# Order of TensorE's products in a fused attention and octonion-FFN block: a planner by runs of one kind, a third p buffer, and ternary signs on ScalarE

## The chip, the cores and the metric

The kernel runs on one core of a Trainium2 chip. The metric is the device time of one execution in microseconds, as the median of several runs. Engines are called by the names of the profile: PE (TensorE's products) and PEld (its weight loads), DVE (VectorE), ACT (ScalarE), POOL (GpSimd) and SP (SyncE, which only issues DMAs here).

## The reference, cut to what matters

Two batches of 1024 tokens with 512 features are normalised once. One branch is a 32-head causal attention with ALiBi, the other an FFN whose three weight matrices are made ternary and expanded by the signs of octonion multiplication. Their product is added to x.

```python
xn = layernorm(x)                                   # x: (2, 1024, 512)
q, k, v = split(xn @ w_qkv.T + b_qkv)               # 32 heads of 16
scores = q @ k.T / 4 + slope[h] * position[k]       # causal: later keys -1e9
s = (softmax(scores) @ v) @ w_out.T + b_out

scale = mean(|W|)                                   # for w_gate, w_up, w_down
Wq = scale * clip(round(W / scale), -1, 1)
M[k, o, i, d] = sum_j S_OCT[j, i, k] * Wq[j, o, d]  # S_OCT has 0, 1 and -1
h = silu(xn @ M_gate) * (xn @ M_up)                 # 1360 wide
g = silu(h @ M_down)
out = x + s * g
```

## The kernel before, in words

**Head (to about 150 us).** Eight tiles of x are loaded by SP, then wv, the FFN weights and eight more tiles. DVE normalises a tile, PE transposes it into PSUM (L358) and ACT copies it to xnT (L359). Meanwhile the FFN weights are made ternary: DVE sums |W| (L264), PE adds over partitions (`tot`, L270), DVE compares with half the scale (L282, L283). For each of the three weights and four slabs `kt`, `expand` (L285 to L304) multiplies by signs: four TENSOR_TENSOR of 340 columns on POOL (L296) into one of two tiles m. `expand_in` then writes m to the DRAM tensor mw by two DMAs that POOL issues (L310, L314); `expand_down` leaves m to PE's transposes (`turn_down`, L328), and ACT copies them on.

**Attention (about 150 to 950 us).** A unit is one batch, one group of four heads and one half of the queries; there are 32 units. Five kinds of product run on PE:
- projections: `pqk` (L433) for q and k, `pv` (L390) for v, `pout` (L667). In fp32, two MATMUL records for one product. q and k are split into a high and a low part, spilled to DRAM and filled back by SP into the rings of tiles q_stack and k_stack.
- scores for the maximum (L501): queries on partitions, 126 rows, into one of two PSUM tiles of pool `ps_x`. DVE reduces each to its row maximum (L511, L514).
- `place_max` (L546): the unit's maxima are transposed by PE, rounded by ACT into `mr` (L553), and written into the last two rows of q_stack by four DMAs that POOL issues (L555). So the next score product subtracts the maximum by itself.
- scores for the exponential (L575): keys on partitions, into one of three PSUM tiles of `ps_e`. On the diagonal a bf16 product of an identity and a mask is added (L584), at once after the score. ACT takes the exponential into p (L585). A cell is one unit and one block of 128 keys, with four heads, so four scores and one tile p.
- value products (L598): p times v, in column tiles of 32, one for each head; a step is the four heads of one cell, eight MATMUL records. At a unit's end `posb`, a transpose (L618) and the normalisation follow.

**Order.** All PE instructions stand in the order in which the program writes them (`pe`, a helper); the tile framework orders the other engines. A planner at build time writes the order: a loop (L927 to L1077) keeps a clock `now`, modelled times of ACT and DVE (`run_act`, `run_dve`), and when PSUM tiles come free (`e_free`, `x_free`, `m_free`). Each round, every source of work (row maxima to place, normalisations, value steps, projections in `side`, FFN transposes in `behind`, scores for the maximum, scores for the exponential) offers its next piece with a ready time and a rank; the earliest wins, and the rank decides among those ready within 60 ns. A change from one kind to another costs nothing in the model. An exponential may be at most one cell ahead of the value steps. Costs are columns times 0.45 to 0.5.

**FFN (from about 953 us).** A fixed loop over four blocks of 512 tokens and eleven slabs `mt`: `gate_up` (L1127), ACT's silu into sg (tag oT), DVE's product h, `down` (L1161), and at each block's end four evictions `ga` (tag mr). The expanded weights come from mw into tiles `fw`, which take over tiles of the attention.

Of the kernel before, what the change touches and what calls it, by code (L numbers as in the profile page):

```python
# [10 lines left out]
F32 = mybir.dt.float32  # L11
# [48 lines left out]
def kernel(  # L60
# [33 lines left out]
    pp = ctx.enter_context(tc.tile_pool(name="pp", bufs=2))  # L94
# [55 lines left out]
    wv_sb = wqp.tile([P, KD, D], F32, tag="wv", name="wv_sb")  # L150
# [25 lines left out]
    nc.sync.dma_start(out=wv_sb, in_=wv.rearrange("(k p) n -> p k n", p=P))  # L176
# [108 lines left out]
    def expand(name, kt, dtype):  # L285

        w = w_tiles[name]
        signs = sgn["d" if name == "d" else "i"]
        m = tmp.tile([P, 8, H8], dtype, tag="m", name=f"m_{name}_{kt}")

        def blocks(t):
            return t.rearrange("p (a b c) o -> p a b c o", a=2, b=2)

        for a in range(2):
            for b in range(2):
                nc.gpsimd.tensor_tensor(  # L296
                    blocks(m)[:, a, b],
                    blocks(w)[:, a ^ (kt // 2), b ^ (kt % 2)],
                    signs[:, kt, 4 * a + 2 * b : 4 * a + 2 * b + 2]
                    .rearrange("p (c o) -> p c o", o=1)  # L300
                    .to_broadcast([P, 2, H8]),
                    ALU.mult,
                )
        return m  # L304
# [72 lines left out]
    def v_items(b, hh):  # L377
# [3 lines left out]
        def product(kt, c):  # L381
# [4 lines left out]
            if c == 0:  # L386
# [6 lines left out]
                    rhs=wv_sb[:, c, hh * 256 : (hh + 1) * 256],  # L393
# [3 lines left out]
            )  # L397
            if c == KD - 1:
                nc.vector.tensor_tensor(  # L399
                    v_tiles[b, hh][:, kt, 0 : 16 * VC].rearrange("p (h e) -> p h e", e=VC)[  # L400
                        :, :, 0:HD
                    ],
                    ps[:, 0:256].rearrange("p (h d) -> p h d", d=HD),
                    bv_sb[:, hh * 256 : (hh + 1) * 256].rearrange("p (h d) -> p h d", d=HD),
                    ALU.add,
                )

        return [
            (1024, lambda kt=kt, c=c: product(kt, c), "v" if c == KD - 1 else None)
# [4 lines left out]
    def qk_items(b, gp):  # L414
# [3 lines left out]
        def product(which, c, kt):  # L418
# [38 lines left out]
            (2048, lambda w=w, c=c, kt=kt: product(w, c, kt), "qk" if kt == KD - 1 else None)  # L457
# [82 lines left out]
    def place_max(b, g, qc, tiles):  # L540
# [11 lines left out]
        mr = wk.tile([8, 512], F32R, tag="mr", name=f"mr_{b}_{g}_{qc}")  # L552
# [12 lines left out]
    def exp_step(b, g, qc, kt, i):  # L565
# [17 lines left out]
        if kt >= 4 * qc:  # L583
            pe(nc.tensor.matmul(ps[:, 0:P], lhsT=ident16, rhs=mask16, start=False, stop=True))  # L584
# [52 lines left out]
    def out_items(b, qc):  # L637
# [53 lines left out]
        for t in range(4 * qc, 4 * qc + 4):  # L691
            if t % 4 == 0:
                items.append((512, lambda t=t: turn(t), "t"))
            if t % 4 < 3:
                items.append((512, lambda t=t: go_on(t), "t"))
            for c in range(KD):
                items.append(
                    (2048, lambda t=t, c=c: product(t, c), "out" if c == KD - 1 else None)
                )
# [111 lines left out]
    def weight(name, last):  # L811
# [6 lines left out]
        later(lambda: ternary_total(name), None, ("s", name), 128)  # L818
# [4 lines left out]
        for kt in range(4):  # L823
# [4 lines left out]
            for f in range(0, NM if last else 0, 4):  # L828
                later(lambda kt=kt, f=f: turn_down(kt, f), None, ("e", name, kt), 512, "t")

    def more_tokens(ts):
        for t in ts:
# [4 lines left out]
            later(lambda t=t: norm_item(t), None, ("n", t), 512, "t")  # L837
# [25 lines left out]
    put([(512, lambda t=t: norm_item(t), "t", ("n", t)) for t in range(4)])  # L863
    put(qk[0:4] + qk[8:12])
    put([(512, lambda t=t: norm_item(t), "t", ("n", t)) for t in range(4, 8)])
# [15 lines left out]
    now = [0.0]  # L881
# [5 lines left out]
    turns, norms = [], []  # L887
    HELD = 1e12
    S_ = [0]

    def take(pool):
        pool.sort()
        return pool

# [32 lines left out]
    while E[0] < len(exps) or V[0] < len(vals) or S_[0] < len(side) or norms or behind:  # L927
        try_fill()
        try_fetch()
# [6 lines left out]
        best = None  # L936

        def offer(ready, rank, go):
            nonlocal best
            start = max(ready, now[0])  # L940
            key = (start if start > now[0] + 60 else now[0], rank)
            if best is None or key < best[0]:
                best = (key, start, go)


        if turns:
            u, ready = turns[0]

            def go(u=u):
                turns.pop(0)  # L950
                place_max(*units[u], mtiles[u])
                now[0] += 500
                take(m_free)[0] = run_act(now[0] + 100, 600)
                placed[u] = m_free[0] + 3500

            offer(max(ready, min(m_free)), 0, go)
        if norms:
            u, ready = norms[0]

            def go(u=u):  # L960
                norms.pop(0)
                normalise(*units[u])
                now[0] += 500
                take(m_free)[0] = run_dve(now[0] + 100, 600)
                stored[units[u]] = m_free[0] + 5000

            offer(max(ready, min(m_free)), 1, go)

        if V[0] < len(vals) and vals[V[0]] in p_ready and (V[0] or S_[0] >= head_v):
            u, kt = vals[V[0]]  # L970

            def go(u=u, kt=kt):
                value_step(*units[u], kt)
                V[0] += 1
                now[0] += 4 * width(units[u][2], kt) * 0.5
                if kt == 4 * units[u][2] + 3:
                    o_free[0] = run_act(now[0] + 100, 600)
                    norms.append((u, o_free[0] + 100))

            vready = p_ready[u, kt] + 100  # L980
            if kt == 0:
                vready = max(vready, o_free[0])
            offer(vready, 2, go)

        if S_[0] < len(side):
            due, ok, (cost, emit, kind, *need) = side[S_[0]]
            if ok():

                def go(cost=cost, emit=emit, kind=kind):
                    emit()  # L990
                    S_[0] += 1
                    now[0] += cost * 0.45
                    if kind == "none":
                        return
                    if HELD not in m_free:
                        take(m_free)[0] = HELD
                    if kind is None:
                        return
                    if kind == "v":
                        end = run_dve(now[0] + 100, 450)  # L1000
                    elif kind == "qk":
                        end = run_dve(run_act(now[0] + 100, 700), 750)
                        done_qk[0] += 1

                        if done_qk[0] == 2 or done_qk[0] % 4 == 0:
                            qk_done.append(end + 4000)
                    elif kind == "t":
                        end = run_act(now[0] + 100, 600)
                    else:
                        end = run_dve(now[0] + 100, 700)  # L1010
                    m_free[m_free.index(HELD)] = end

                t = 0 if HELD in m_free or not cost else min(m_free)
                for k in need:
                    t = max(t, known[k] + 100)
                offer(t, 3 if pos >= due else 6, go)

        while behind and not behind[0][3] and known.get(behind[0][2], 0) <= now[0]:
            emit, model = behind.pop(0)[:2]
            emit()  # L1020
            if model:
                model()
        if behind and behind[0][3]:
            emit, model, need, cost, kind = behind[0]

            def go(emit=emit, cost=cost, kind=kind):
                behind.pop(0)
                emit()
                now[0] += cost * 0.45
                if kind == "t":  # L1030
                    take(m_free)[0] = run_act(now[0] + 100, 600)

            offer(max(known[need] + 100, 0 if HELD in m_free else min(m_free)), 4.5, go)

        if M[0] < len(maxs):
            u, n, count, cost, emit = maxs[M[0]]
            g = u // 2
            if fills[0] > 4 * g + 1 + 2 * units[u][2] and (n or u < 2 or u - 2 in placed):
                mpos = at[u] + (at[u + 1] - at[u]) * n / count

                def go(u=u, n=n, count=count, cost=cost, emit=emit):
                    emit()
                    M[0] += 1
                    now[0] += cost * 0.46
                    end = run_dve(now[0] + 100, cost * 1.1 + 190)
                    take(x_free)[0] = end
                    if n == count - 1:
                        split_max(*units[u], mtiles[u])
                        turns.append((u, run_dve(end, 400) + 100))

                lead = size[1] + size[0] * 0.6
                rank = 4 if mpos < pos + lead else 5.5
# [235 lines left out]
```

## Time and profile before

| | |
|---|---|
| median of 3 runs | 1231.95 us (1231.39 to 1234.6) |
| profiled execution | 1228.66 us |
| its span, first to last instruction | 1226.9 us |
| granted PE clock over the span | 0.963 |
| L585, exponentials on ACT, x768 | 332.2 us busy |
| L501, scores for the maximum, x768 | 312.3 us busy |
| L575, scores for the exponential, x768 | 255.5 us busy |
| L598, value products, x1536 | 166.4 us busy |
| L433, q and k projections, x256 | 137.0 us busy |
| L584, masks, x512 | 115.6 us busy |
| L555, DMAs of the maxima, issue to landing | 1.6 us median |
| L310, DMAs of the expanded weights | 5.3 us median |

The page gives for each engine its busy time, share of the span and number of instructions; a chain of work that ended last; and groups of equal instructions. A line of the timeline has the start and the length in us, the engine, the line of the kernel, the operation, output and inputs by name, and the shapes. Times of one line overlap with those of the next: PE's ends are modelled, and a product's record may start while its weights are still being loaded. Intervals between starts are therefore more telling than lengths.

### The profile page before, as it was taken

To read this page: it belongs to the slowest core of one execution; us is meant where nothing else is said; L and a number is where in the kernel's file an instruction comes from. 1 tells how busy PE (TensorE), PEld (TensorE's weight loads), DVE (VectorE), ACT (ScalarE), POOL (GpSimd) and SP (SyncE) were. 2 spreads that over 40 slices of the span, in tenths; PEclk is the share of its full clock that TensorE was granted. 3 is DMA by queue.
4 is the path that set the end of the run, shared out by engine and by line. 5 is a ranking of instruction groups with operands and counts; after the bars stand their busy time and mean duration, and the time that the engine had idled before them with its cause. 6 is when DMAs were issued, how large, how long until landed. Compare 5 with 4: busy or idle time off the path is not lost.

```text
span 1226.9 us, 16539 instructions
## 1 busy us (share of the span) xinstructions
PE 1117.5 (91%) x5714; PEld 671.7 (55%) x5714; DVE 617.5 (50%) x1640; ACT 487.0 (40%) x1035; POOL 272.8 (22%) x446
## 2 busy tenths in 40 slices
PE   4757689989999999998999999999888999999997
PEld 2534445544455555545555554455444677777775
DVE  6684327656666665665655655666641113232122
ACT  1113252445546445453544534455453212222222
POOL 6697430200210110012001000100110113232222
PEclk9887889999999998999999999999889999999999
DMA  9963484163544152533616332652316110203020
GB/s 277 239 191 121 132 118 93 36 114 54 129 64 69 47 127 47 90 75 92 97 60 114 53 88 50 141 81 49 108 49 205 44 61 14 89 9 95 9 95 35
DMA packets 76788, 112.31 MB, mean 92 GB/s; under 512 B 29424, under 2 KB 30960, under 8 KB 76704
## 3 DMA queue, kind: packets, MB, share of 16 engines
q1 hardware_dynamic: 67120, 93.05, 34.2%
q0 software_dynamic: 9296, 17.16, 5.0%
q8 instruction: 45, 0.74, 0.3%
q10 hardware_dynamic: 288, 1.05, 0.2%
q14 instruction: 39, 0.32, 0.1%
HBM read 72.71 MB, written 37.98 MB: 90 GB/s over the span
## 4 chain that ended last, share of the span: by engine, by line
PE 76%; DMA 7%; POOL 6%; issue 6%; DVE 3%; ACT 2%; SPq 0%; DVEq 0%; POOLq 0%; ACTq 0%
PE s L501 14%; PE s L575 13%; PE po L598 12%; PE pg L1127 7%; PE pqk L433 6%; PE pu L1127 6%; PE pd L1161 6%; PE pout L667 4%; DMA q_stack<-mr 4%; PE s L584 3%; PE pv L390 2%; DVE scr L514 1%; PE pm L546 1%; POOL m_g L296 1%; PE pt L618 1%
## 5 line engine op out<-in xcount | busy, mean ns | idle before, releaser
L585 ACT ACTIVATE p<-s 128x512 f32<-128x512 f32 (+3 forms) x768 | 332.2, 493 | 323.2 <-PE s L584 174.6
L501 PE MATMUL s<-k_stack,q_stack 126*128 126x512 f32 (+3 forms) x768 | 312.3, 448 | 6.3 <-DVE mx L514 4.2
L575 PE MATMUL s<-q_stack,k_stack 128*128 128x512 f32 (+3 forms) x768 | 255.5, 391 | 32.0 <-DMA q_stack<-mr 30.2
L501 PEld LDWEIGHTS s<-k_stack,q_stack 126*128 126x128 f32 x768 | 138.4, 194 | 164.6 <-DVE mx L514 74.1
L511 DVE TENSOR_REDUCE mp<-s 128x1 f32<-128x512 f32 x256 | 170.2, 688 | 81.9 <-PE s L501 80.1
L514 DVE CUSTOM_DVE_ANT_0 scr<-s,mask,mp 128x128 f32<-128x128 f32 (+3 forms) x256 | 140.7, 550 | 106.7 <-PE s L501 93.1
L575 PEld LDWEIGHTS s<-q_stack,k_stack 128*128 128x128 f32 x768 | 151.0, 199 | 70.1 <-DMA q_stack<-mr 35.0
L555 POOL DMA_DIRECT2D q_stack<-mr x128 | 63.9, 505 | 520.4 <-ACT mr L553 455.2
L514 DVE CUSTOM_DVE_ANT_0 scr<-s,mask 128x128 f32<-128x128 f32 (+3 forms) x256 | 125.2, 489 | 91.6 <-PE s L501 74.4
L598 PE MATMUL po<-p,v 128*32 128x512 f32 (+3 forms) x1536 | 166.4, 502 | 0.0
L433 PE MATMUL pqk<-xnT,wq 128*128 128x512 f32 x256 | 137.0, 637 | 16.3 <-ACT mr L553 10.6
L1138 DVE SCALAR_TENSOR_TENSOR h<-pu,sc_u,sg 128x512 f32<-128x512 f32 (+1 forms) x44 | 33.0, 750 | 166.1 <-PE pu L1127 156.3
L584 PE MATMUL s<-mask,ident 128*128 128x128 bf16 x512 | 115.6, 231 | 0.0
L1144 POOL TENSOR_TENSOR hs<-h,hs 128x512 fp32r<-128x512 f32 (+1 forms) x44 | 56.9, 1293 | 197.2 <-ACT hs L1143 197.2
L584 PEld LDWEIGHTS <-ident 128*128 128x128 bf16 x512 | 49.4, 96 | 56.9 <-issue 37.4
L390 PE MATMUL pv<-wv_sb,xnT 128*128 128x256 f32 x256 | 72.6, 395 | 2.6 <-DVE v L399 1.2
L433 PEld LDWEIGHTS pqk<-xnT,wq 128*128 128x128 f32 x256 | 47.2, 203 | 41.5 <-issue 19.5
L1136 ACT ACTIVATE sg<-pg,sc_g 128x512 f32<-128x512 f32 (+1 forms) x44 | 30.3, 688 | 97.9 <-PE pg L1127 97.8
L667 PE MATMUL pout<-wo_sb,oT 128*128 128x512 f32 x128 | 62.4, 602 | 1.7 <-ACT oT L658 1.0
L598 PEld LDWEIGHTS po<-p,v 128*32 128x32 f32 x1536 | 31.4, 108 | 58.0 <-issue 51.5
L1143 ACT CAST hs<-h 128x512 fp32r<-128x512 f32 (+1 forms) x44 | 27.3, 621 | 77.7 <-DVE h L1138 74.9
L390 PEld LDWEIGHTS pv<-wv_sb,xnT 128*128 128x128 f32 x256 | 45.1, 194 | 13.6 <-issue 4.5
(147 smaller groups left out, 1127.0 us busy)
## 6 DMA issues: line engine op xcount, KB each, us to landing
sp<-st SPq DMA_DIRECT2D x32, 512.0 KB
k_stack<-sp SPq DMA_DIRECT2D x128, 128.0 KB
q_stack<-sp SPq DMA_DIRECT2D x128, 128.0 KB
wqr<-in_wqk_dram POOLq DMA_DIRECT2D x14, 512.0 KB, 6.1
xt<-in_x_dram SPq DMA_DIRECT2D x16, 256.0 KB
att<-o SPq DMA_DIRECT2D x32, 128.0 KB
ot<-att SPq DMA_DIRECT2D x16, 256.0 KB
proj<-y SPq DMA_DIRECT2D x16, 256.0 KB
```

What stands on the lines that cost most here:

```text
L390: nc.tensor.matmul(ps[:, 0:256], lhsT=xnT[:, c, b * S + kt * P : b * S + (kt + 1) * P], rhs=wv_sb[:, c, hh * 256 : (hh + 1) * 256], start= ...
L433: nc.tensor.matmul(ps, lhsT=wq_tiles[b, gp][:, kt, which, :], rhs=xnT[:, kt, b * S + c * 512 : b * S + (c + 1) * 512], start=(kt == 0), st ...
L501: nc.tensor.matmul(ps[:, :n], lhsT=q_of(b, g, qc)[0 : NR - 2, i, tl * P : (tl + 1) * P], rhs=k_of(b, g, c)[0 : NR - 2, i, :n], start=True, ...
L511: nc.vector.tensor_reduce(pm, ps, AX.X, ALU.max)
L514: nc.vector.tensor_tensor_reduce(out=scr[:, :n], in0=ps[:, :n], in1=mask[:, 512 - n : 512], scale=1.0, scalar=pm if qc else -3.0e38, op0=A ...
L575: nc.tensor.matmul(ps[:, :w], lhsT=k[0:NR, i, kt % 4 * P : (kt % 4 + 1) * P], rhs=q[0:NR, i, 512 - w : 512], start=True, stop=(kt < 4 * qc),)
L584: pe(nc.tensor.matmul(ps[:, 0:P], lhsT=ident16, rhs=mask16, start=False, stop=True))
L585: nc.scalar.activation(p_tiles[b, g, qc, kt][:, i, :w], ps[:, :w], AF.Exp, scale=0.25)
L598: nc.tensor.matmul(po[32 * i : 32 * i + 32, 512 - w : 512], lhsT=v[:, kt, h * VC : h * VC + 32], rhs=pr[:, i, :w], start=(kt == 0), stop=( ...
L667: nc.tensor.matmul(ps, lhsT=turned[t][:, c, :], rhs=wo_sb[:, c, :], start=(c == 0), stop=(c == KD - 1),)
L1127: nc.tensor.matmul(ps[:fs, :], lhsT=fw[mt][:, n0 + kt, 0:fs], rhs=part[:, kt, :], start=(kt == 0 and n == 0), stop=(kt == KD - 1 and n == 1),)
L1161: nc.tensor.matmul(pd, lhsT=hs[k][:fs, n, st * P : (st + 1) * P], rhs=fw[mt][:fs, 8:12, :].rearrange("p s n -> p (s n)"), start=(mt == 0 a ...
```

## The change

Edits that the text speaks of:
- PE's kinds get letters: R (both scores), V (value), F (fp32), B (bf16 mask). A table SWITCH charges changes of kind. Costs are set anew (858 for a 512-column projection product in place of 2048 times 0.45, and so on).
- The planner goes on with scores while one can start soon. When none can, it writes all masks that are pending, and only then their exponentials. Then come value steps and other work, with a budget RUN for side work, before the next scores.
- A value step of even key block waits in the model for the next cell too, so that two steps come together. The exponentials may be two cells ahead, and p has three tiles.
- `expand` is eight ACTIVATEs with the sign as scale, of 170 columns, on ACT.
- wv is loaded in halves of 256 columns, four times in all, into one buffer; the next half is issued after the last product that reads the one before.
- `mr` has one buffer, `ga` takes the tag oT, and the third FFN weight tile takes over a p tile.

```diff
-    pp = ctx.enter_context(tc.tile_pool(name="pp", bufs=2))
+    pp = ctx.enter_context(tc.tile_pool(name="pp", bufs=3))
...
-    wv_sb = wqp.tile([P, KD, D], F32, tag="wv", name="wv_sb")
+    wv_tiles = {}
+    def load_wv(n):
+        w = wqp.tile([P, KD, D // 2], F32, tag="wv", name=f"wv_{n}")
+        nc.sync.dma_start(
+            out=w,
+            in_=wv.rearrange("(k p) n -> p k n", p=P)[:, :, n % 2 * 256 : n % 2 * 256 + 256],
+        )
+        wv_tiles[n] = w
...
-        for a in range(2):
-            for b in range(2):
-                nc.gpsimd.tensor_tensor(
-                    blocks(m)[:, a, b],
-                    blocks(w)[:, a ^ (kt // 2), b ^ (kt % 2)],
-                    signs[:, kt, 4 * a + 2 * b : 4 * a + 2 * b + 2]
-                    .rearrange("p (c o) -> p c o", o=1)
-                    .to_broadcast([P, 2, H8]),
-                    ALU.mult,
-                )
+        for k in range(8):
+            nc.scalar.activation(
+                m[:, k, :], w[:, k ^ kt * 2, :], AF.Identity, scale=signs[:, kt, k : k + 1]
+            )
...
+            if (kt, c) == (7, KD - 1) and 2 * b + hh < 2 * B - 1:
+                load_wv(2 * b + hh + 1)
...
-        if kt >= 4 * qc:
-            pe(nc.tensor.matmul(ps[:, 0:P], lhsT=ident16, rhs=mask16, start=False, stop=True))
+        return ps
+
+    def mask_step(ps):
+        pe(nc.tensor.matmul(ps[:, 0:P], lhsT=ident16, rhs=mask16, start=False, stop=True))
+
+    def exp_of(b, g, qc, kt, i, ps):
+        w = width(qc, kt)
         nc.scalar.activation(p_tiles[b, g, qc, kt][:, i, :w], ps[:, :w], AF.Exp, scale=0.25)
...
+    SWITCH = {
+        ("R", "V"): 95,
+        ("F", "V"): 95,
+        ("B", "V"): 95,
+        ("V", "R"): 200,
+        ("V", "F"): 100,
+        ("V", "B"): 95,
+        ("R", "B"): 60,
+        ("F", "B"): 95,
+        ("B", "R"): 105,
+        ("B", "F"): 50,
+    }
+    SOON = 80
+    RUN = 1800
...
+    def run_pe(k, ready, cost):
+        now[0] = max(ready, now[0] + SWITCH.get((kind[0], k), 0)) + cost
+        kind[0] = k
...
+    def next_exp():
...
+        if u not in placed or V[0] < E[0] // 4 - 2:
+            return []
...
+        def go():
+            ps = exp_step(*units[u], kt, i)
+            E[0] += 1
+            run_pe("R", ready, max(width(units[u][2], kt) * 0.417 + 18, 108))
+            take(e_free)[0] = HELD
+            if kt < 4 * units[u][2]:
+                after(ps)
+            else:
+                masks.append((ps, after))
...
+    def next_value():
...
+        if kt % 2 == 0 and E[0] < len(exps) and E[0] // 4 < V[0] + 3:
+            ready = max(ready, p_ready.get((u, kt + 1), HELD) - 800)
+        return [(ready, 0, 0, go)] if ready < HELD else []
...
+        def soon(found):
+            return [f for f in found if f[0] <= now[0] + SOON and f[1] < 7]
+
+        scores = next_max(pos) + next_exp()
+        scores.sort(key=lambda f: (max(f[0], now[0] + SOON), f[1]))
+        if kind[0] == "R" and soon(scores):
+            scores[0][3]()
+            return True
+        if masks:
+            run_pe("B", 0, 60)
+            ps, after = masks.pop(0)
+            mask_step(ps)
+            after(ps)
+            return True
+        rest = next_value() + next_turn() + next_side(pos) + next_behind()
+        rest.sort(key=lambda f: (max(f[0], now[0] + SOON), f[1]))
+        if soon(rest) and (left[0] > 0 or not soon(scores)):
+            left[0] -= rest[0][2]
+            rest[0][3]()
+            return True
+        left[0] = RUN
+        found = soon(scores) or scores + rest
...
-        wqp.tile([P, 12, P], F32R, tag="wv", name="fw_2"),
+        pp.tile([P, 4, 512], F32R, tag="p", name="fw_2"),
...
-            ga = wk.tile([P, D], F32, tag="mr", name=f"ga_{n}")
+            ga = wk.tile([P, D], F32, tag="oT", name=f"ga_{n}")
```

## The prediction

> **What bounds the kernel now.** I read the page first, then the stretches of 100 us, PE's waits, and the timeline of PE alone.
>
> ```profile
> span 1226.9 us, 16539 instructions
> PE 1117.5 (91%) x5714; PEld 671.7 (55%) x5714; DVE 617.5 (50%) x1640; ACT 487.0 (40%) x1035; POOL 272.8 (22%) x446
> ...
> PE 76%; DMA 7%; POOL 6%; issue 6%; DVE 3%; ACT 2%; SPq 0%; DVEq 0%; POOLq 0%; ACTq 0%
> ```
>
> ```profile
> 0.00:100.00 100.00, 61.15 (x199) 36.89 (x199) 70.91 (x138) 17.26 (x37) 74.08 (x161) 0.88 0.84 234
> ...
> 300.00:400.00 100.00, 98.29 (x596) 53.67 (x594) 68.81 (x202) 53.06 (x121) 13.06 (x27) 1.00 0.52 92
> ```
>
> The columns of the second fence are the stretch, then PE, PEld, DVE, ACT and POOL busy. PE is the bound from about 150 us on; the first 150 us are a chain of several engines. DVE at 69 and ACT at 53 of 100 us have room. But a busy PE is not a PE multiplying: the timeline shows what passes between its products.
>
> ```profile
> 303.57 0.33 PE L575 MATMUL s<-q_stack,k_stack 128*128 128x384 f32 x1
> 303.75 0.23 PE L584 MATMUL s<-mask,ident 128*128 128x128 bf16 x1
> 303.79 0.42 PE L575 MATMUL s<-q_stack,k_stack 128*128 128x384 f32 x1
> 304.05 0.23 PE L584 MATMUL s<-mask,ident 128*128 128x128 bf16 x1
> 304.21 1.07 PE L598 MATMUL po<-p,v 128*32 128x512 f32 x8
> 305.20 0.61 PE L501 MATMUL s<-k_stack,q_stack 126*128 126x384 f32 x2
> 305.65 0.34 PE L575 MATMUL s<-q_stack,k_stack 128*128 128x384 f32 x1
> 305.83 0.23 PE L584 MATMUL s<-mask,ident 128*128 128x128 bf16 x1
> ```
>
> Durations overlap in these records, so I use steps from start to start. I name the kinds E (score for the exponential, L575), M (score for the maximum, L501), B (mask, L584), V (value, L598) and F (projections and transposes).
> - **A mask.** From mask to mask over one 384-wide E: 304.05 − 303.75 = 0.30 us. A 384-wide M or E without a mask behind it takes 0.177 (the short steps of these products). So E's companion costs 0.123 us, where its own 128 columns are about 0.06 (a quarter of the 0.235 step of 512 columns, below): 0.063 is change of kind.
> - **A value step.** Its second pass starts 0.45 after the first, and all its columns need 0.86. Over the whole trace, the median from the product before to the second pass is 0.115 us more than the products themselves, and from the last pass to the second product after it 0.216 us more. Together 0.33 us per visit to V.
> - **M after M** never steps below 0.335 us at 512 columns; E after E steps at 0.235 (median of 133). So 0.104 us each.
>
> From 150 to 935 us (785 us) the products alone, at their undisturbed steps, are 270 (M, E) + 178 (F) + 130 (V) + 30 (B) = 608. Add 188 visits to V × 0.33 = 62, 496 masks × 0.063 = 31, 215 × 0.104 = 22, and 41 of waits that the wait view lists: 764. Only 21 us stay unexplained. The largest wait is
>
> ```profile
> PE s L575 <- DMA q_stack<-mr: 23.5, 8, 6.2
> ```
>
> **What the Trainium skill says.** TensorEngine Tiling (Array Packing), Key Properties: a change of tiling mode drains TensorE. V runs in 32-column tiles, everything else on the full array; the 0.33 us agrees. TensorE: Matmul & The Clock Gate, Step-by-step: weight loads are pulled ahead of running matmuls. E after E (0.235) agrees, M after M (0.335) doesn't show it. ScalarE: Activation LUTs, What ACT_TABLE_LOAD costs: an ACTIVATE takes 186 ns + 0.833 per element, 93 more per pointer operand, and neighbours overlap by 93; four 512-wide exponentials in 2.08 us (0.52 each) agree. GPSIMD Engine Reference, Specifications: it shares SBUF interfaces with VectorE; at 74.39 us a 128x16 CAST on DVE (L537) takes 5.35 us beside POOL's memset and sign products, which fits.
>
> **The change, part by part.** The built program's order of PE can be counted, before against after. The products are the same: 768 M, 768 E, 512 B, 768 V, 751 F.
> 1. *Visits to V* fall from 192 (always one step) to 103 (89 of two steps). 89 × 0.33 = 29.4 saved; two steps in one visit keep a pass-to-pass step, 89 × 0.021 = 1.9. Net −27.5. They lie on PE, the bound; nothing else covers them.
> 2. *Runs of masks* fall from 512 to 217 (134 of three). 295 changes go. A mask behind a mask isn't in this trace: at best 0.053 us (128 columns), at worst 0.107 (its weight load, 0.096 busy, not hidden). Saved per mask: 0.123 − 0.053 = 0.070 down to 0.016; sums −20.7 to −4.7. I take 0.06 per mask in a run, since the load is of another matrix than the running product needs: 295 × 0.063 = −18.6.
> 3. *M after M* rises from 222 to 243: +2.2.
> 4. *The wait for q_stack<-mr.* It comes where the row maxima are placed shortly ahead of the unit's first E. Summing PE's product and change times between the two in both orders: for the 18 units with little between, 5.3 us on average before and 5.0 after. The others have 13 to 25 us. The wait stays; 0.3 × 8 waits = 2.4, taken as +3, bounds 0 and +8.
> 5. *Masks in batches, three p.* An exponential now starts only after its batch's masks, and ACT's queue behind it waits with it. Three score buffers are held meanwhile. PE has about 3 us of other work per three tiles (E 0.5, masks 0.3, M 0.7, V 0.55, F 0.9), ACT needs 1.2 to 1.5. The third p lets E run two cells ahead of V instead of one. I take +3; −5 (part of the 21 goes) to +20.
> 6. *Signs on ACT.* 48 POOL products of 0.75 us (36 us) go; 96 ACTIVATEs come. Estimate from the ScalarE page: 170 columns and one pointer, 186 + 142 + 93 − 93 = 0.33 us each, 2.6 per slab, 32 in all; ACT has 83 of its first 100 us free. A slab's two DMAs stay on POOL, 5.3 us from issue to landing, and two m buffers exist, so slab 3 of ACT waits for slab 1's DMA. With w_g ready at 54.5 as before, slabs start at 54.5, 57, 63, 66, 71, 74, 80, 83. In ACT's order the first xnT copy of tiles 8 to 11 stands behind slab 7: about 82 instead of 61.3. PE's next projection needs that copy's PSUM bank: 17 us idle. Then PE catches up without the 10.0 us wait at 82 to 92 of before; the first two w_d slabs and four square roots precede mr: mr at 107 (before 91.6). POOL is now free: four DMAs at once (before queued until 104.5), first E near 111 against 106.1. But by then PE has done 58 us of products against 53. Net 0; bounds −6 (DVE and POOL disturbed less, −11 at most at the first E, half of it kept) and +10 (DMA later than the median).
> 7. *Small ones.* wv comes in four halves on SP (512 KB each instead of 1 MB once); each waits for PE's last read of the half before, and SP's spills and fills queue behind it only for that product. The next reader comes several us later. ga shares sg's buffers and mr has one: at most one eviction, 0.7 us, for each of four token blocks. fw_2 in the third p is needed 11 us into the last stage. Together +1, 0 to 3.
>
> Sum: −27.5 − 18.6 + 2.2 + 3 + 3 + 0 + 1 = −37. The profiled execution took 1228.66 us (span 1226.9 and 1.8 around it) and would take 1192; the median of the runs is 1231.95, 3.3 above it, so I predict 1195.
>
> **Rivals.**
> *A: a mask in a run costs nearly what it did* (0.107): 14 less saved. With 168 more steps from E to M, whose 512-wide median is 260 instead of 231 ns, 5 more: −18, 1214. For it: weight loads of 0.19 us that PE can't always pull ahead. Against: E after E hides them.
> *B: the head gains too.* DVE and POOL no longer disturb each other, the first E comes 11 us earlier, and the fuller model shrinks the q_stack waits by 8: −56, 1176. For it: the 5.35 us CAST, and POOL's queue ahead of q_stack<-mr until 104.5. Against: the two m buffers now stall ACT.
> *C, slower: the batch starves ACT and then PE.* In a batch of three the first exponential starts later by two E steps and a change, 2 × 0.177 + 0.06 = 0.41 us; in a batch of two by 0.24. If no other work covers it: 134 × 0.41 + 27 × 0.24 = 61, and −37 becomes +24: 1256. It decides from 37 / 161 = 0.23 us exposed per batch. For it: three score buffers, all in the batch. Against: ACT idle 323 us ahead of its exponentials, and PE's wait for p totals 0.8 us.
> That the change doesn't do what it says is excluded by the counts of 1 and 2.
>
> **How the numbers follow.** Forecast 0.62 (1180 to 1208), A 0.18, B 0.10, C 0.08, the head alone losing more than is saved 0.02. The range from 1174 to 1220 leaves out C and the tails of B and A. Faster by over 0.3% (about what a measurement of this kernel can tell from no change): all of the forecast and B, nearly all of A: 0.88; within 0.03; slower 0.09.
>
> **What would show it.** Right: visits to V and mask runs cost the same 0.33 and 0.123 as before, the stretch from the first E of unit 1 (157 us) to the last value step is 40 to 45 us shorter, the stage of the last 270 us is unchanged, mask-to-mask steps near 0.06. Wrong: steps near 0.11 (A); waits for p or for s on L575's counterpart beyond 10 us (C); the first E far from 106 to 112 (part 6 or B).

## The result and the profile after

The changed kernel takes 1227.82 us (median; 1220.8 to 1234.24) against 1231.95 of the kernel before: a ratio of the means of 0.9958, with a 95% interval of 0.9941 to 0.9975, or 5 us less (the medians differ by 4). Forecast were 1195 us, 37 less. The profiled execution of after lies at the low end of its runs.

The page of after, the lines that answer to those of before:

```profile
span 1220.9 us, 16626 instructions
PE 1094.6 (90%) x5714; PEld 686.8 (56%) x5714; DVE 600.5 (49%) x1640; ACT 508.3 (42%) x1131; POOL 233.1 (19%) x398
...
PE 69%; DMA 10%; DVE 7%; issue 5%; POOL 4%; ACT 4%; SPq 0%; DVEq 0%; ACTq 0%; POOLq 0%
```

PE's busy time fell by 23 us, the span by 6. The chain of waits tells what came instead: DVE's share rises from 3% to 7%, DMA's from 7% to 10%, ACT's from 2% to 4%. The stretches of 100 us of after:

```profile
0.00:100.00 100.00, 50.36 (x168) 32.70 (x169) 44.23 (x101) 34.60 (x92) 45.31 (x127) 0.83 0.84 220
300.00:400.00 100.00, 89.36 (x542) 53.09 (x540) 62.53 (x189) 47.95 (x112) 12.96 (x27) 0.93 0.38 69
```

Cut by stage instead (to unit 1's first E, to the last value step, to the end), first before, then after; the columns are as in the prediction:

```profile
0.00:157.40 157.40, 96.38 (x383) 60.03 (x383) 90.33 (x188) 36.04 (x77) 106.88 (x212) 0.86 0.69 189
157.40:934.10 776.70, 742.81 (x4176) 400.44 (x4176) 461.45 (x1375) 377.08 (x844) 88.74 (x177) 0.97 0.42 83
934.10:1226.90 292.80, 278.35 (x1158) 211.25 (x1156) 65.73 (x77) 73.83 (x114) 77.17 (x59) 0.99 0.19 61
```

```profile
0.00:156.90 156.90, 93.69 (x375) 58.63 (x375) 77.68 (x188) 65.37 (x171) 62.97 (x160) 0.85 0.68 186
156.90:925.90 769.00, 720.84 (x4184) 416.10 (x4184) 457.43 (x1375) 368.93 (x847) 92.69 (x181) 0.98 0.42 86
925.90:1220.90 295.00, 280.10 (x1156) 212.02 (x1156) 65.40 (x77) 73.97 (x114) 77.44 (x59) 0.99 0.19 62
```

The stage that was to lose 40 to 45 us lost 7.7, though PE is busy 22 us less in it. Three further traces with the very same order of PE's products (two are shown below) have 775.0, 777.0 and 773.9 us there, so 7.7 is the best of four. The head is as long as before, the last stage 2.2 us longer.

PE's timeline of after shows that the changes of kind did go:

```profile
402.35 0.70 PE L504 MATMUL s<-k_stack,q_stack 126*128 126x384 f32 x2
402.89 0.82 PE L578 MATMUL s<-q_stack,k_stack 128*128 128x384 f32 x3
403.55 0.34 PE L589 MATMUL s<-mask,ident 128*128 128x128 bf16 x3
403.71 0.50 PE L504 MATMUL s<-k_stack,q_stack 126*128 126x512 f32 x1
404.05 0.60 PE L391 MATMUL pv<-wv,xnT 128*128 128x256 f32 x2
404.58 1.71 PE L606 MATMUL po<-p,v 128*32 128x512 f32 x16
406.22 0.73 PE L504 MATMUL s<-k_stack,q_stack 126*128 126x512 f32 x2
```

Three masks take 0.34 us where one took 0.23: 0.055 for each mask behind a mask, so rival A is out. Two value steps share one visit (x16). But the E run from 402.89 to the mask at 403.55 has three products of 0.177 = 0.53 in 0.66 us: the third's bank came free at 403.22 only, and its load started at 403.27. Ahead of it, two M and three E are five products in a row, as many as there are PSUM tiles for scores. In PE's order, 100 runs of scores are exactly five long; before, runs of one and two were the rule (545 of 727).

**Where PE's time beyond its products goes.** For each step from start to start in the stage I took the excess over the undisturbed step, and sorted it: beside a visit to V (with the step after it), beside a mask, between scores, at a score product that stood behind its *own bank* (its load starts within 0.11 us of the eviction that frees its PSUM tile, and it comes late), other products, and waits over 1 us together with stretches at half clock. In us, for the main kernels of the text:

| | V | mask | scores | own bank, E | own bank, M | other | waits, half clock | sum |
|---|---|---|---|---|---|---|---|---|
| before | 60.6 | 12.1 | 10.5 | 13.0 | 17.9 | 17.4 | 45.2 | 176.6 |
| after | 31.1 | 7.5 | 11.1 | 18.9 | 32.1 | 21.3 | 46.0 | 168.0 |
| after, each mask at once | 31.6 | 12.1 | 18.5 | 8.4 | 32.3 | 21.8 | 52.8 | 177.6 |
| after, no pairs | 56.6 | 5.1 | 7.1 | 16.3 | 30.2 | 18.9 | 51.1 | 185.2 |
| before, halved evictions | 62.0 | 11.1 | 10.4 | 8.3 | 3.9 | 17.0 | 52.9 | 165.6 |
| after, halved evictions | 31.6 | 3.1 | 8.9 | 9.5 | 8.9 | 17.8 | 74.8 | 154.6 |
| after halved, no pairs | 55.6 | 0.7 | 8.2 | 9.2 | 8.9 | 16.6 | 61.3 | 160.4 |
| after, banks reckoned free later | 30.9 | 6.3 | 7.9 | 12.7 | 31.5 | 18.2 | 49.2 | 156.7 |
| that, signs on POOL, ga in ot | 30.9 | 6.2 | 9.1 | 13.7 | 30.0 | 18.2 | 45.9 | 153.8 |
| the line above, no pairs | 59.3 | 3.4 | 6.1 | 10.2 | 29.5 | 20.0 | 37.5 | 165.9 |

V gives 29.5 us and masks 4.6, and 20.1 come back at the scores' own banks. Loads within 0.11 us of their bank's release: 110 of E and 225 of M before, 214 and 319 after. This repeats: the three further traces with after's order have 528 to 533 together, the one with before's order 334. PEld's waits from 200 to 930 us show E's part; first before, then after (total, times, longest):

```profile
PEld s L501 <- DVE mx L514: 71.4, 160, 2.6
...
PEld s L575 <- ACT p L585: 15.3, 50, 0.8
```

```profile
PEld s L504 <- DVE mx L517: 49.8, 154, 2.3
...
PEld s L578 <- ACT p L593: 26.6, 98, 0.9
```

E's loads wait twice as often for ACT. M's idle time falls in this view, but the view puts all idle time ahead of a load down to the last release in it: 51 of the 160 waits of before, 38.2 us, are loads that follow a visit to V, and their bank had been free for 1.0 us (median). Of these waits, those whose load starts within 0.11 us of its bank's release rise from 29.4 us (93) to 42.0 (126). That is why the sorting above goes by PE's steps.

**The head.** PE's largest waits of after, and ACT's timeline there:

```profile
PE pv L391 <- ACT xnT L360: 23.8, 1, 23.8
PE s L578 <- DMA q_stack<-mr: 19.0, 15, 5.9
```

```profile
57.55 5.34 ACT L302 ACTIVATE m_g<-w_g,sgn_i 128x170 fp32r<-128x170 f32 x16 [5.92 <-DVE w_g L293]
70.05 5.34 ACT L302 ACTIVATE m_g<-w_g,sgn_i 128x170 fp32r<-128x170 f32 x16 [7.15 <-DMA mw<-m_g]
77.92 5.34 ACT L302 ACTIVATE m_u<-w_u,sgn_i 128x170 fp32r<-128x170 f32 x16 [2.54 <-DMA mw<-m_g]
85.68 2.73 ACT L302 ACTIVATE m_u<-w_u,sgn_i 128x170 fp32r<-128x170 f32 x8 [2.42 <-DMA mw<-m_u]
88.31 0.56 ACT L360 COPY xnT<-ptx 128x512 f32<-128x512 f32 x1
```

A slab takes 2.67 us (two in 5.34), as worked out. But the first slab starts 3 us later than reckoned (57.55 against 54.5), the slabs wait 12 us for the DMAs that free their buffers, where the reckoned starts leave 9, and the copy that PE needs comes at 88.3 us instead of 82.

### The profile page after: what moved, and what is told of

Read it like the earlier page. It is cut to its first block, busy times and chain, and to the rows that moved or that the text cites. A ratio compares the mean times of both kernels' runs of the same rounds, so it can differ in the third digit from the quotient of the medians.

```text
span 1220.9 us, 16626 instructions
## 1 busy us (share of the span) xinstructions
PE 1094.6 (90%) x5714; PEld 686.8 (56%) x5714; DVE 600.5 (49%) x1640; ACT 508.3 (42%) x1131; POOL 233.1 (19%) x398
## 4 chain that ended last, share of the span: by engine, by line
PE 69%; DMA 10%; DVE 7%; issue 5%; POOL 4%; ACT 4%; SPq 0%; DVEq 0%; ACTq 0%; POOLq 0%
PE s L578 12%; PE s L504 12%; PE po L606 11%; PE pqk L436 6%; PE pg L1206 6%; PE pu L1206 5%; PE pd L1240 5%; DMA q_stack<-mr 5%; PE pout L675 4%; DVE scr L517 3%; PE pv L391 2%; PE s L589 2%; PE pm L549 1%; DVE mp L514 1%; DMA mw<-m_g 1%
## 5 line engine op out<-in xcount | busy, mean ns | idle before, releaser
L593 ACT ACTIVATE p<-s 128x512 f32<-128x512 f32 (+3 forms) x768 | 323.4, 495 | 313.9 <-PE s L589 217.1
L504 PE MATMUL s<-k_stack,q_stack 126*128 126x512 f32 (+3 forms) x768 | 306.6, 439 | 13.5 <-DVE mx L517 5.6
L578 PE MATMUL s<-q_stack,k_stack 128*128 128x512 f32 (+3 forms) x768 | 248.6, 388 | 25.4 <-DMA q_stack<-mr 19.0
L578 PEld LDWEIGHTS s<-q_stack,k_stack 128*128 128x128 f32 x768 | 141.9, 193 | 96.9 <-ACT p L593 33.1
L606 PE MATMUL po<-p,v 128*32 128x512 f32 (+3 forms) x1536 | 148.2, 498 | 0.0
L436 PE MATMUL pqk<-xnT,wq 128*128 128x512 f32 x256 | 135.2, 632 | 12.7 <-ACT mr L556 6.0
L391 PE MATMUL pv<-wv,xnT 128*128 128x256 f32 x256 | 74.6, 399 | 25.0 <-ACT xnT L360 23.8
L606 PEld LDWEIGHTS po<-p,v 128*32 128x32 f32 x1536 | 42.8, 110 | 65.8 <-issue 55.5
L589 PE MATMUL s<-mask,ident 128*128 128x128 bf16 x512 | 66.7, 225 | 0.0
L391 PEld LDWEIGHTS pv<-wv,xnT 128*128 128x128 f32 x256 | 45.1, 194 | 34.5 <-ACT xnT L360 24.2
L449 DVE SCALAR_TENSOR_TENSOR st<-pqk,bqk_sb,st 128x512 fp32r<-128x512 f32 x32 | 23.8, 747 | 45.1 <-ACT st L448 44.9
```

Source lines behind the costliest of these rows:

```text
L391: nc.tensor.matmul(ps[:, 0:256], lhsT=xnT[:, c, b * S + kt * P : b * S + (kt + 1) * P], rhs=wv_tiles[2 * b + hh][:, c, :], start=(c == 0), ...
L436: nc.tensor.matmul(ps, lhsT=wq_tiles[b, gp][:, kt, which, :], rhs=xnT[:, kt, b * S + c * 512 : b * S + (c + 1) * 512], start=(kt == 0), st ...
L504: nc.tensor.matmul(ps[:, :n], lhsT=q_of(b, g, qc)[0 : NR - 2, i, tl * P : (tl + 1) * P], rhs=k_of(b, g, c)[0 : NR - 2, i, :n], start=True, ...
L578: nc.tensor.matmul(ps[:, :w], lhsT=k[0:NR, i, kt % 4 * P : (kt % 4 + 1) * P], rhs=q[0:NR, i, 512 - w : 512], start=True, stop=(kt < 4 * qc),)
L593: nc.scalar.activation(p_tiles[b, g, qc, kt][:, i, :w], ps[:, :w], AF.Exp, scale=0.25)
L606: nc.tensor.matmul(po[32 * i : 32 * i + 32, 512 - w : 512], lhsT=v[:, kt, h * VC : h * VC + 32], rhs=pr[:, i, :w], start=(kt == 0), stop=( ...
```

## Experiments

Theories (a bank is one PSUM tile for scores). *Banks:* longer runs of scores run into the five score banks, which DVE and ACT free at their own pace; the changes of kind had covered that time. *Price* (rival): the changes never cost what I reckoned. *Head* (rival): the stage's gain is lost to the signs on ACT. Differences between kernels are differences of their ratios to the kernel before, times 1232 us; each ratio's interval is about 2 to 3 us to either side.

**Undoing one part at a time.**

```diff
# signs back on POOL: the four nc.gpsimd.tensor_tensor of before
-                masks.append((ps, after))          # each mask at once
+                mask_step(ps)
+                masks.append((ps, after))
...
-            mask_step(ps)
             after(ps)
...
-        if kt % 2 == 0 and E[0] < len(exps) and E[0] // 4 < V[0] + 3:     # no pairs
-            ready = max(ready, p_ready.get((u, kt + 1), HELD) - 800)
```

> The changed kernel with the sign products back on POOL, everything else as changed. Head theory (what the attention stage gained was lost in the head, where xnT's copy stands behind the sign slabs on ACT and PE idles 23.8 us): the wait goes and the kernel takes 1221 us or less, 7 or more under the changed kernel's 1228. Bank theory (runs of score products catch up with their five PSUM banks) and price theory (the changes of kind never cost what I reckoned): the head is worth little, 1226 to 1230, as part 6 of the prediction has it (net 0).

> The changed kernel with each mask right behind its score product on PE (512 runs of masks in place of 217); the order of all else, the exponentials' too, is kept. Price on record (0.063 us for each of 295 changes): 18.6 us slower than the changed kernel, 1246. Price theory (the mean excess of a mask in the trace of before is 0.047 us, its waits included): at most 295 x 0.047 = 14 slower, 1234 to 1242. Bank theory: the time between score products lets DVE and ACT free their banks, so that most of it is covered: 1228 to 1234.

> The changed kernel without the rule that two value steps go together: 184 visits to V in place of 103. Price on record (0.33 us for each of 81 visits): 27 us slower than the changed kernel, 1254. Bank theory: a visit to V is time in which the score banks come free, so the waits of score products that come after it shrink and only about half is paid: 1236 to 1243. Head theory: as the price on record.

> The kernel before with the sign products on ACT, nothing else changed. Part 6 of the prediction and the bank theory: within 3 us of 1232. Head theory: 7 or more slower, 1239 and above.

| | median, us | ratio, 95% interval | against |
|---|---|---|---|
| signs on POOL | 1217.49 | 0.9877 (0.9854 to 0.9900) | after: −10 |
| each mask at once | 1227.34 | 0.9963 (0.9951 to 0.9975) | after: +0.6 |
| no pairs | 1240.84 | 1.0072 (1.0056 to 1.0089) | after: +14 |
| before, signs on ACT | 1236.05 | 1.0028 (1.0012 to 1.0043) | before: +3.4 |

Batches are worth nothing, pairs half their price, signs on ACT cost 10 us in the new order and 3.4 in the old one. −14 − 0.6 + 10 = −4.6, against the −5 of the result; but each part was undone alone and they need not add up, so the match is no proof. Head and price are each partly right. The stage in the traces of signs on POOL, and of these with `ga` in ot (below):

```profile
145.00:920.00 775.00, 725.93 (x4184) 418.87 (x4184) 457.34 (x1375) 369.54 (x847) 93.66 (x183) 0.97 0.43 85
144.50:921.50 777.00, 724.59 (x4184) 418.44 (x4184) 457.30 (x1375) 368.68 (x847) 93.58 (x183) 0.97 0.43 85
```

Unit 1's first E comes 12 us earlier than in after, and the stage is 6 to 8 us longer than in after's quick trace.

The table of excesses says more. Without pairs, V loses 25.5 us more, the price on record (81 × 0.33 = 27), but masks, scores and banks lose 10.9 less. A visit to V is time in which banks come free: of the scores right behind a visit, 1 of 171 before and 2 of 81 after stood at their own bank. Yet only 4.5 of the 10.9 lie at own banks. With each mask at once masks and scores lose 12 more, and E's banks 10.5 less: the batch holds all three of E's tiles until its masks are done.

**Faster evictions.** PE's products and order unchanged; DVE takes the maximum over every second column, ACT half an exponential, with the exponent's scale at 0.001. The rest of p is set to 1 once by POOL, so these kernels leave half of the softmax out.

```diff
-                nc.vector.tensor_reduce(pm, ps, AX.X, ALU.max)
+                nc.vector.tensor_reduce(pm, ps[:, 0:512:2], AX.X, ALU.max)
...
-        nc.scalar.activation(p_tiles[b, g, qc, kt][:, i, :w], ps[:, :w], AF.Exp, scale=0.25)
+        nc.scalar.activation(p_tiles[b, g, qc, kt][:, i, : w // 2], ps[:, : w // 2], AF.Exp, scale=0.001)
```

> The kernel before, with DVE taking the maximum over every second column of a score product and ACT the exponential of half its columns (the rest of p is set to 1 once by POOL; the exponent's scale is 0.001 instead of 0.25), so that the five score banks come free sooner; PE's products and their order are the same. In the trace of before, score products whose load starts within 110 ns of the release of their own bank lose 35 us. Bank theory: most of that goes, 1200 to 1212. Price theory: PE's order alone sets the time, 1225 to 1232.

> The changed kernel with the same halved maxima and exponentials. Its score products lose 56 us behind their own banks, 21 more than before. Bank theory: the gap to the kernel before, halved in the same way, grows from 5 to 17 us or more. Price theory: the gap stays at 5.

> The changed kernel with each mask right behind its score product (exponentials' order kept) and the same halved maxima and exponentials. With full evictions the batches were worth 0.6 us: 8 saved on masks, 7 lost to score products behind the exponentials' banks. Bank theory: with the banks free sooner the batches are worth 6 us or more against the halved changed kernel. Price theory: still 0 to 2.

> The changed kernel without pairs of value steps and with the same halved maxima and exponentials. With full evictions the 81 visits more cost 14 us where 27 were on record. Bank theory: 20 to 28 more than the halved changed kernel. Price theory: 14 again.

Before 1219.03 (0.9895, 0.9878 to 0.9911), after 1207.94 (0.9799, 0.9773 to 0.9825), each mask at once 1218.67 (0.9893, 0.9875 to 0.9911), no pairs 1212.07 (0.9838, 0.9814 to 0.9863). Before lies between what the two theories expected. The gap of after to before grows from 5 to 12 us, and batches are worth 11.6 where they were worth 0.6: for banks, against price. The own-bank excess of after is 6 us above before's here, where it was 20. But the gap stays under the 17 expected, and pairs are worth 5, less than the 14: against both.

The table shows why: PE now runs into waits over 1 us, above all for the maxima's DMA, and into half clock (74.8 us, against 61.3 without pairs and 52.9 of before). One of these waits is the experiment's own: ACT stands 10.6 us behind POOL's setting of p. The rest says that a bound that is lifted uncovers the next. Nor is the grown gap all banks: in these two traces 13.3 us of it lie in the head (unit 1's first E at 162.1 us before and 148.8 after) and 10.4 in the stage, where it was 7.7. And after's profile is the quickest of its five runs, by 4 us or more; the others had a mean clock of 0.951 to 0.953 against its 0.960, so half clock cost them more.

**The head's mechanism, the last stage, the third p.** DVE copies xnT for tiles 8 to 11; `ga` gets the tag ot, unused in the last stage, with the signs on POOL; the planner holds E to one cell ahead of V, and the rule on pairs goes with it.

```diff
+        if 8 <= t < 12:
+            nc.vector.tensor_copy(xnT[:, :, t * P : (t + 1) * P], pt)
...
-            ga = wk.tile([P, D], F32, tag="oT", name=f"ga_{n}")
+            ga = wk.tile([P, D], F32, tag="ot", name=f"ga_{n}")
...
-        if u not in placed or V[0] < E[0] // 4 - 2:
+        if u not in placed or V[0] < E[0] // 4 - 1:
...
-        if kt % 2 == 0 and E[0] < len(exps) and E[0] // 4 < V[0] + 3:
+        if kt % 2 == 0 and E[0] < len(exps) and E[0] // 4 < V[0] + 2:
```

> The changed kernel, signs on ACT, but the four PSUM copies into xnT for tiles 8 to 11 on DVE. Head theory in the form that the first such copy, held behind ACT's sign slabs (23.8 us of idle PE), is what costs 10 us: the wait goes and 5 to 10 come back, 1218 to 1223. Rival: mr, behind the w_d slabs on the same queue, sets the first exponential anyway: 1225 to 1228.

> The changed kernel with the signs back on POOL, and with the last stage's ga in ot's two buffers, which nothing else uses there, in place of oT's, which sg uses. In the traces the last stage (first to last gate product) takes 265.6 us before and 270.3 after. If ga's shared buffers are the cause: 3 to 4.5 us less than with the signs on POOL alone (1217.5), 1213 to 1214.5. If it is something else (fw_2 in p, or nothing but scatter): no difference.

> The changed kernel, planned as if p had two buffers (a score product for the exponential at most one tile ahead of the value step, as before; 126 visits to V in place of 103). Visits at the 0.17 us that undoing the pairs showed: 23 x 0.17 = 4 more, 1232. If the third p also keeps PE from waiting for p or for the exponentials: 1236 to 1245. If the third p is worth nothing beyond the pairs: 1230 to 1233.

DVE's copies: 1222.34 (0.9917, 0.9896 to 0.9938), 5 us of the 10. The wait of 23.8 is gone, another comes up: DVE's st waits 16.5 us for ACT's st, which stands behind the same slabs, and PE waits for DVE (PE's waits of this kernel):

```profile
PE tot_d L280 <- DVE st L452: 16.5, 1, 16.5
```

`ga` in ot: 1214.66 (0.9853, 0.9833 to 0.9873), 3 us less than signs on POOL alone. In the waits of after ACT's sg stands behind y, since `ga` holds one of sg's two buffers; with ot this line is gone, and the last stage is 292.3 us, as before the change:

```profile
ACT sg L1215 <- DVE y L1255: 4.9, 3, 1.6
```

Planned for two p: 1222.46 (0.9922, 0.9898 to 0.9946), 4 us less than after, if anything (the intervals just touch), though V is visited 126 times: against all three expectations. So letting E run two cells ahead brings nothing here. This kernel still has three p tiles; none was run with two.

**Banks reckoned free later.** If products are placed right behind a release, the planner should be told that a bank is free later. It took 60 ns after the eviction.

```diff
-            take(x_free)[0] = end + 60
+            take(x_free)[0] = end + 160
...
-            e_free[e_free.index(HELD)] = end + 60
+            e_free[e_free.index(HELD)] = end + 160
```

> Signs on POOL, ga in ot's buffers, and the planner reckons each score bank free 0.1 us later than the change has it (160 in place of 60 ns after the eviction), since a score product whose load starts right at the release pays about 0.1 us for the load. Bank theory: fewer products are placed right behind a release, 3 to 6 us less than with the same kernel without this, 1208 to 1212. Rival (the waits are set by DVE's and ACT's speed and can't be planned away): no difference, 1212 to 1216.

> The changed kernel with one number of the planner changed in two places: a score bank counts as free 160 ns after its eviction instead of 60. Bank theory: as with the signs on POOL, about 20 us less than the changed kernel, 1204 to 1212. Rival (orders scatter, the gain was luck): no reason for the same size; anything from 1215 to 1235.

> Signs on POOL, ga in ot's buffers, banks reckoned free 110 ns after the eviction (60: 1214.7, 160: 1192.6). Bank theory: between the two, 1198 to 1210. Rival (scatter): anything from 1205 to 1225.

> The same with 260 ns. Bank theory: the release and the load together take about 0.25 us, so no loss against 160: 1188 to 1198. Rival (scatter): 1205 to 1225.

> The same with 160 ns for the maximum's two banks alone, 60 for the exponential's three. By the trace DVE's banks hold back 32 of 51 us: bank theory 1198 to 1206. If the exponential's banks matter as much: above 1206. Rival (scatter): 1205 to 1225.

| | median, us | ratio, 95% interval | against 60 ns |
|---|---|---|---|
| POOL, ot, 160 ns | 1192.59 | 0.9689 (0.9664 to 0.9714) | −20 |
| after, 160 ns alone | 1203.87 | 0.9770 (0.9749 to 0.9790) | −23 |
| POOL, ot, 110 ns | 1190.95 | 0.9679 (0.9657 to 0.9701) | −21 |
| POOL, ot, 260 ns | 1191.69 | 0.9685 (0.9672 to 0.9697) | −21 |
| POOL, ot, 160 ns for M's banks alone | 1210.68 | 0.9829 (0.9811 to 0.9847) | −3 (intervals overlap) |

The first of these kernels was expected to gain 3 to 6 us and gained 20. That is beyond the scatter of orders that these runs show: four kernels with three orders gain 20 to 23 us, where the two other small edits of the planner (one cell ahead, M's banks alone) gave 3 to 4. One number in the changed kernel brings most of what was forecast. But it is a step, not a slope (110 does as much as 260, and more than was expected of it), and M's banks alone bring 3 of it, short of the bank theory (E's alone were not tried).

In the profile of the second kernel the head is 7.7 us shorter and the stage is the first line here; the second line is the stage of the first kernel:

```profile
149.20:906.90 757.70, 720.98 (x4184) 424.94 (x4184) 459.41 (x1375) 371.37 (x848) 93.85 (x183) 0.96 0.44 87
142.70:897.60 754.90, 718.48 (x4185) 423.11 (x4184) 459.66 (x1375) 371.86 (x848) 93.69 (x183) 0.97 0.44 87
```

The first is 11.3 us shorter than after's, at the same PE busy time. The table gives 6.8 of that to own banks, 7.5 to masks, scores and other products, and 3.2 back to waits and half clock. The second is 22 us shorter than with the signs on POOL, `ga` in ot and 60 ns (777.0 us, above). The loads within 0.11 us of their bank's release fall from 533 to 475 only, and of runs of exactly five scores there are 115 where there were 100, so the length of the runs alone isn't the harm. The later reckoning didn't take most products from behind their banks, it bettered the order in several places at once; which of them counts most, and how it shortens the head of the one kernel, stays open.

**The parts in that better order** (POOL, ot, 160 ns):

> Signs on POOL, ga in ot's buffers, banks reckoned free 160 ns after the eviction (1192.6), without the rule on pairs of value steps: 186 visits in place of 102. If the parts get their own price once the banks are reckoned right: 84 x 0.33 = 28 slower, 1214 to 1222. If later banks gain for another reason, the pairs stay at the 14 of the changed kernel: 1204 to 1209.

> The same with each mask right behind its score product on PE, the order of all else kept. If the batches get their own price (8 us of excess beside the masks in the trace, 11.6 with halved evictions): 1200 to 1205. If they stay at the 0.6 of the changed kernel: 1191 to 1195.

No pairs: 1205.71 (0.9789, 0.9767 to 0.9811), 12 us more. Each mask at once: 1201.09 (0.9738, 0.9707 to 0.9769), 6 more, give or take 4. The batches now seem to pay; the pairs still pay half, as expected if the later banks gain for another reason. In this trace V loses 28.4 us more without pairs, the full price; banks, masks and scores lose 10 less, waits and half clock 8.4 less.

The quickest kernel, signs on POOL, `ga` in ot and 110 ns, takes 1190.95 us, 41 less than before.

## Why the prediction was wrong, step by step

Three steps failed: masks were priced too high (2), the wait for banks, +20.1 us, was taken as +3 (5), and the visits' price was taken as paid in full (1). That the head came out as forecast is luck (6).

1. *Visits to V, −27.5.* The price was right: −29.5 in the trace. What failed is "nothing else covers them": undone alone, the pairs are worth 14. Waits for banks are part of what a visit hides (4.5 us in the trace without pairs). They aren't all of it, since with halved evictions the pairs are worth 5 and not more; the rest of the cover stays open.
2. *Masks, −18.6.* This step failed in size. The 0.063 us came from one pair of steps at 304 us; over the stage, outside bank waits and half clock, the 496 masks of before lose 12.1 us, 0.024 each. Grouping saves 4.6 beside masks, at most 12 with the scores after them, and E's banks take 10.5 of that back. Worth: 0.6.
3. *M after M, +2.2.* Between scores with a free bank the trace gives +0.6. (Before, the shortest step at 512 columns is 0.313 us, not 0.335.)
4. *q_stack<-mr, +3.* Its waits fell from 30.2 to 19.0 us over the kernel; waits over 1 us and half clock together rose by 0.8, in a quick execution of after.
5. *Batches and three p, +3, bounds −5 and +20.* This is the term that should have held the banks' wait: +20.1. I looked for starved exponentials (rival C) and averaged engines over three tiles; the 533 loads at their bank's release, 335 before, show that PE often takes a bank just as it comes free, though DVE and ACT are busy only 60% and 48% of the stage.
6. *Signs, net 0.* The head's length is right (157.4 to 156.9), its working isn't: the copy at 88.3 and not 82, first E at 122.6 and not 111. With signs on POOL unit 1's first E comes at 145.0 (the first E of all at 109.8, no earlier than before). So the rest of the change shortens the head by 12 us, about as much as rival B had hoped for from ACT's taking the signs, and the slabs on ACT take 12 back. In the median the signs cost 10 us, the upper bound of this step and not its 0; the net 0 is luck.
7. *Small ones, +1.* +2.2, almost all `ga`'s shared buffer.

Other products took 3.9 more. With 0.9 us more of products in the stage, −29.5 − 4.6 + 0.6 + 0.8 + 20.1 + 3.9 + 0.9 − 0.5 + 2.2 = −6.1, the span's −6.0. This closes the sum for this pair of executions; the other traces of the same order (stage of 774 to 777 us) show how far single ones lie apart.

## What to carry to other kernels

Before you count the removal of small gaps on the busiest engine as gain, ask what else happens in a gap: here the gaps gave two other engines time to free PSUM, and more than half of what was removed in the trace came back as waits that PE's own wait view doesn't list, because the engine counts as busy. Take the price of a change from the mean over the whole trace, not from one clean example. When a planner orders work by modelled times, an error of 0.05 to 0.1 us in when a buffer is free can be worth more than the rule the planner was given.

## What the hardware showed unexpectedly

A wait can be paid twice. After's PE in two neighbouring stretches (the last but two columns is the granted clock):

```profile
318.80:322.20 3.40, 1.98 (x10) 1.21 (x10) 2.31 (x15) 0.57 (x1) 2.75 (x7) 1.00 1.10 140
322.20:335.90 13.70, 7.71 (x16) 4.92 (x17) 5.23 (x18) 3.09 (x6) 0.78 (x2) 0.50 0.83 187
```

PE was busy 1.98 of 3.40 us, and then had half the clock for 13.7 us. In five traces (before, after, and three with later banks) every stretch at half clock in the stage follows 3.4 us with PE at most 76% busy, and lasts a multiple of 3.4 us. The reverse doesn't hold: in after's stage six such windows with PE 51% to 61% busy were followed by full clock, so the busy share alone doesn't decide. The Trainium skill, TensorE: Matmul & The Clock Gate, What's actually happening, has the half clock after an idle window of about 3.4 us; here a window needn't be idle, a thin one can be enough. Each kernel lost 16 to 36 us of its stage's clock this way (half of its time at half clock). That is likely part of why executions of one kernel differ by several us: over the 20 runs of after, longer time goes with lower mean clock (correlation −0.73).

A score that stands behind another, and whose load starts right at its bank's release, comes 0.106 us late in the median (422 in after). M after M with the load ahead shows 0.002 us over the undisturbed step (38 in after), so M after M isn't slow in itself, as the prediction took it to be. In the other 192 the load is late. In 98 of them it starts at its own bank's release (0.32 us, median). In 94 the bank had been free for longer (0.77 us), and 0.106 is lost all the same: nearly always (90) the product ahead had started with its own load, and the next load starts only 0.11 us behind that one. Before the change this second kind is the rule, 160 of 215.
